# Experts' groups and the router's normalisation moved to ScalarE, and the seams around the last batch's dense experts rearranged

## The chip, the cores and the metric

The kernel runs on one core of one Trainium2 chip. A core has five engines with separate in-order queues: TensorE (PE, with its weight loads PEld) multiplies matrices, VectorE (DVE) and ScalarE (ACT) do elementwise work and read PSUM, GpSimd (POOL) does elementwise work in SBUF and issues indirect DMAs, and SyncE (SP) issues the other DMAs. They meet at semaphores. The metric is the device time of one execution in microseconds (us); the time before is the median of three runs.

## The reference

A hybrid layer of four sublayers on x of shape 4 x 1024 x 128 (4096 tokens, 128 features), each added back to x after a layer norm of its input:

```python
x = x + attn_a(layernorm(x))   # causal softmax attention, 16 heads of 64
x = x + ffn(layernorm(x))      # 32 experts, top 2
x = x + attn_b(layernorm(x))   # linear attention, 16 heads of 8
x = x + ffn(layernorm(x))      # the same experts again

def layernorm(x):
    return (x - mean(x)) / sqrt(var(x) + 1e-5)

def ffn(x):
    rw = softmax(x @ router_w.T)                 # 32 weights a token
    w = rw where it is one of the 2 largest, else 0
    return sum over e of (x * w[:, e]) @ expert_w[e]

def attn_b(x):
    q, k, v = x @ Wq.T, x @ Wk.T, x @ Wv.T
    g = sigmoid(x @ Wg.T + bg)
    qf, kf = softplus(q) * (g + 1e-6), softplus(k)
    kv_cum, z_cum = cumsum(kf x v), cumsum(kf)   # over the 1024 tokens
    return ((qf . kv_cum) / (qf . z_cum + 1e-6)) @ Wo.T
```

All of it is in float32.

## The kernel before

x stays in SBUF for the whole program, as 32 chunks of 128 tokens (x_sb; eight chunks a batch, four chunks a quarter q). Four stages follow one another.

**Softmax attention** (lines 477 to 834). A loop over 4 batches and 8 pairs of heads; for each pair eight units, one per chunk of queries. The function slot issues one unit's scores and, in between, later steps of earlier units. project returns a generator of six pieces (two halves of keys and queries, two pieces of values) that fill the slots of the pair before; for the very first pair all six are run ahead of the loop (lines 723 to 725). Sparse experts of a finished batch run beside it: experts (line 197) sorts tokens by expert through DRAM, and its last step, fetch (line 438), adds the results back with 16 indirect DMAs that POOL issues from a queue, one each time the queue is popped. At the end project_out (line 704) adds the last batch's output into x_sb chunk by chunk, and statistics (line 117) takes mean and variance of four chunks at a time and returns mean and reciprocal deviation.

**Dense experts of the last batch** (lines 1115 to 1145, names ending in _f). routed (line 851) prepares a quarter: normalised rows xn (VectorE, line 873), their transposes pxn (line 884), the copy xnT (line 885), router logits pl (line 892), softmax and the two largest weights, w. dense (line 928) then multiplies every token by all 32 experts. A block is a pair of chunks (c0 = 0 or 2) and eight groups g of four experts; each group takes two PSUM tiles of 512. For the groups in ACT_GROUPS (1, 4, 6) ScalarE multiplies by the weight into an SBUF tile t (line 966) and POOL adds the tiles of a chunk together (line 972), folding four experts into one at the end of a block (lines 990 and 991). For the other five groups VectorE multiplies and adds into x_sb straight from PSUM (line 978). settle (line 934) adds the folded partial sums to x_sb (line 937) when a later block has begun, and all that are left at the end of dense. Twice in each group dense calls next on the routing of the following quarter and beside(turn), so there are 16 turns in a block; for a quarter whose statistics are known, its routing is over within the first block.

Beside these blocks run the first two preparations of the linear stage, prepare (line 1018), for batch 0's chunks 0 to 3 and 4 to 7: statistics, reciprocal deviation rstd and negated product nb on POOL, normalised rows on ScalarE (line 1039), transposes, four projections pj (line 1057) with four ScalarE copies each, Exp, Sigmoid, Ln, and POOL's sums. In fill the two preparations advance in turn, and every fourth turn pops one item of the queue, which holds the fetches of batch 2's sparse experts.

**Linear attention** (lines 1147 to 1248). For each chunk u: cumulate (line 1158) multiplies kv by a triangular matrix into three PSUM banks, outputs (line 1175) makes the products m on VectorE, carry (line 1167) completes the running sum, finish divides, projects and adds. products (line 1095) makes the next chunk's kv on POOL. Preparations run 26 thirds of a chunk ahead.

**Experts after it** (lines 1250 to 1272, names ending in _s). Batch 0's quarters go through sparse experts beside dense on the quarters 2 to 7, twelve blocks. Here statistics are not known in advance, so routed takes them itself, with rstd on POOL (line 864), and its steps spread over the first block and half of the second. At the end of dense the results go out by DMA (line 940).

From line 847 on the program's order within each engine is that of the Python code (manual_schedule), so an instruction that waits holds everything that was written after it for the same engine.

Of the kernel before, what the change touches and what calls it, by code (L numbers as in the profile page):

```python
# [8 lines left out]
F32 = mybir.dt.float32  # L9
# [6 lines left out]
P = 128  # L16
# [4 lines left out]
def hybrid_kernel(  # L21
# [95 lines left out]
    def statistics(c0, n, nm):  # L117

        st = small.tile([P, n, nc.vector.BN_STATS_DIM], F32, tag=f"st{n}", name=f"st_{nm}")
        mv = small.tile([P, n, nc.vector.BN_AGGR_DIM], F32, tag=f"mv{n}", name=f"mv_{nm}")  # L120
        for c in range(n):
            nc.vector.bn_stats(st[:, c, :], x_sb[:, c0 + c, :])
            nc.vector.bn_aggr(mv[:, c, :], st[:, c, :])
        ve = small.tile([P, n], F32, tag=f"ve{n}", name=f"ve_{nm}")
        nc.vector.tensor_scalar_add(ve, mv[:, :, 1], LN_EPS)
        rstd = small.tile([P, n], F32, tag=f"rstd{n}", name=f"rstd_{nm}")
        nc.gpsimd.tensor_tensor(rstd, ve, mhalf[:, :n], ALU.pow)
        return mv, rstd
# [345 lines left out]

    sides, queue = [], []
    banks = [None]
    with attn as ph:
# [245 lines left out]
        cur, ahead = project(0, 0)  # L723
        for _ in ahead:
            pass
# [69 lines left out]
        for i, (b, pr) in enumerate(pairs):  # L795
# [10 lines left out]
            for k, ib in enumerate(ORDER):  # L806
# [12 lines left out]
                slot(u, (nm, ib - 1, twos[two], va, oT), k)  # L819
            if i + 1 < len(pairs):  # L820
                cur = nxt
# [9 lines left out]
        for c, _ in enumerate(project_out(*pend)):  # L831
            if c % 4 == 3:
                c0 = (B - 1) * NB + c - 3
                known.append(statistics(c0, 4, f"mf_{c0 // 4}"))

# [9 lines left out]
    ACT_GROUPS = (1, 4, 6)  # L845
# [5 lines left out]
    def routed(q, nm, pool, known=None):  # L851

        c0 = q * 4
        if known is None:
# [9 lines left out]
            nc.gpsimd.tensor_tensor(rstd, ve, mhalf[:, :4], ALU.pow)  # L864
            yield
            yield
            yield
        else:
            mv, rstd = known
        xn = rp.tile([P, 4, D], F32, tag="xn", name=f"xn_{nm}")  # L870
        xnT = rp.tile([P, 4 * P], F32, tag="xnT", name=f"xnT_{nm}")
        for c in range(4):
            nc.vector.tensor_scalar(
                xn[:, c, :], x_sb[:, c0 + c, :], mv[:, c, 0:1], rstd[:, c : c + 1],
                ALU.subtract, ALU.mult,
# [52 lines left out]
    def dense(nm_, qs, store, pool, mp, ps_e, known, beside):  # L928
# [16 lines left out]
        for i, q in enumerate(qs):  # L945
# [4 lines left out]
            for c0 in (0, 2):  # L950
                parts = [[], []]
                for g in range(E // 4):
# [9 lines left out]
                    if g in ACT_GROUPS:  # L962
# [32 lines left out]
        settle(0)  # L995
# [5 lines left out]

    lin = ExitStack()
# [3 lines left out]
    G = 4  # L1006
# [4 lines left out]
    tri, eps = mtri, epsn[:, :G]  # L1011
# [3 lines left out]

    feats = {}

    def prepare(t, pool):

        c0 = t * G  # L1020
        st = small.tile([P, G, nc.vector.BN_STATS_DIM], F32, tag="stl", bufs=2, name=f"st_l{t}")
        mv = small.tile([P, G, nc.vector.BN_AGGR_DIM], F32, tag="mvl", bufs=2, name=f"mv_l{t}")
        for c in range(G):
            nc.vector.bn_stats(st[:, c, :], x_sb[:, c0 + c, :])
            nc.vector.bn_aggr(mv[:, c, :], st[:, c, :])
            if c == 1:
                yield
        rstd = small.tile([P, G], F32, tag="rstdl", bufs=2, name=f"rstd_l{t}")
        nb = small.tile([P, G], F32, tag="nbl", bufs=2, name=f"nb_l{t}")
        nc.gpsimd.tensor_tensor(rstd, mv[:, :, 1], eps, ALU.add)  # L1030
        nc.gpsimd.tensor_tensor(rstd, rstd, mhalf[:, :G], ALU.pow)
        nc.gpsimd.tensor_tensor(nb, mv[:, :, 0], rstd, ALU.mult)
        nc.gpsimd.tensor_scalar(nb, nb, -1.0, None, ALU.mult)
        yield
        yield
        xn = lb.tile([P, G, D], F32, tag="xn", bufs=2, name=f"xn_l{t}")
        xnT = lb.tile([P, G * P], F32, tag="xnT", bufs=2, name=f"xnT_l{t}")
        for c in range(G):
            nc.scalar.activation(
                xn[:, c, :], x_sb[:, c0 + c, :], AF.Identity,  # L1040
                scale=rstd[:, c : c + 1], bias=nb[:, c : c + 1],
            )
        yield
        pt = pool.tile([P, 512], F32, tag="ps1", name=f"pxn_l{t}")
        for c in range(G):
            nc.tensor.transpose(pt[:, c * P : (c + 1) * P], xn[:, c, :], ident)
        nc.scalar.copy(xnT, pt)
        yield
        kq = lb.tile([P, G, 2 * P], F32, tag="kq", name=f"kq_{t}")
        y = lb.tile([P, G, 2 * P], F32, tag="y", bufs=2, name=f"y_{t}")  # L1050
        u = lb.tile([P, G, 2 * P], F32, tag="u", bufs=2, name=f"u_{t}")
        ln = lb.tile([P, G, 2 * P], F32, tag="ln", bufs=2, name=f"ln_{t}")
        gt = lb.tile([P, G, P], F32, tag="gt", bufs=2, name=f"gt_{t}")
        va = lb.tile([P, G, P], F32, tag="va", name=f"va_{t}")
        for c in range(G):
            pj = pool.tile([P, 512], F32, tag="ps1", name=f"pj_{t}_{c}")
            nc.tensor.matmul(
                pj, xnT[:, c * P : (c + 1) * P], wc.rearrange("p w d -> p (w d)"),
                start=True, stop=True,
            )  # L1060
            nc.scalar.activation(y[:, c, :], pj[:, : 2 * P], AF.Abs)
            nc.scalar.activation(kq[:, c, :], pj[:, : 2 * P], AF.Relu)
            nc.scalar.copy(gt[:, c, :], pj[:, 2 * P : 3 * P])
            nc.scalar.copy(va[:, c, :], pj[:, 3 * P :])
            if c == G - 1:
                nc.gpsimd.tensor_tensor(
                    gt, gt, bg_sb.unsqueeze(1).to_broadcast([P, G, P]), ALU.add
                )
            yield


        nc.scalar.activation(y, y, AF.Exp, scale=-1.0)
        nc.scalar.activation(u, y, AF.Copy, bias=1.0)
        yield
        yield
        nc.scalar.activation(gt, gt, AF.Sigmoid)
        yield
        yield
        nc.vector.scalar_tensor_tensor(y, u, 1.0, y, ALU.subtract, ALU.subtract)
        nc.scalar.activation(ln, u, AF.Ln)  # L1080
        yield
        yield
        yield
        for i in range(2):
            cols = slice(i * P, (i + 1) * P)
            nc.gpsimd.tensor_tensor(ln[:, :, cols], ln[:, :, cols], y[:, :, cols], ALU.subtract)
            nc.gpsimd.tensor_tensor(kq[:, :, cols], kq[:, :, cols], ln[:, :, cols], ALU.add)
            yield
        yield
        yield  # L1090
        q = kq[:, :, P:]
        nc.vector.scalar_tensor_tensor(q, gt, 1e-6, q, ALU.add, ALU.mult)
        feats[t] = (kq, va)
# [21 lines left out]
    with ExitStack() as ph:  # L1115
        mp = ph.enter_context(tc.tile_pool(name="mpf", bufs=12, reuse_waits="tile"))
# [3 lines left out]
        preps = [prepare(t, ps_f) for t in range(2)]  # L1120

        def fill(turn):

            if turn == 56:
# [5 lines left out]
            if turn % 4 == 3:  # L1130
# [5 lines left out]
        for _ in routed(qs[0], f"f_{qs[0]}", ps_f, known[0]):  # L1136
            next(preps[0], None)
        dense("f", qs, False, ps_f, mp, ps_e, known, fill)
# [8 lines left out]
    with lin as ph:  # L1147
# [80 lines left out]
        for u in range(NT + 4):  # L1228
# [15 lines left out]
            ahead(3 * u + 2)  # L1244
            if u == NT - 8:
# [3 lines left out]

    for _ in first:  # L1250
        pass
# [11 lines left out]
    with ExitStack() as ph:  # L1263
# [4 lines left out]
        dense("s", qs, True, ps_s, mp, ps_e, [None] * len(qs), pieces)  # L1268
# [36 lines left out]
```

## Time and profile before

| what | value |
|---|---|
| time, median of 3 runs (lowest, highest) | 2023.33 us (2021.16, 2025.43) |
| profiled execution: its time | 2022.32 us |
| its span, first to last instruction | 2020.6 us |
| mean granted TensorE clock | 0.980 |
| busy: PE, DVE, ACT, POOL | 1887.1, 1500.4, 1228.5, 1136.2 us |
| DMA, mean over the span | 31 GB/s |

The stages by the first and last instructions of their lines:

| stage | from | to |
|---|---|---|
| first scores to last residual add of softmax attention | 22.5 | 1479.7 |
| dense experts of the last batch, matmuls | 1495.5 | 1569.8 |
| linear attention, first to last running sum | 1577.0 | 1769.1 |
| dense experts after it, matmuls | 1773.4 | 2013.2 |

A row of the profile's timeline gives start, duration, engine, line, operation, the tiles written and read, shapes, and in brackets how long the engine had been idle and what ended that. A row of the table by stretches gives for each engine the busy time and the number of instructions, then the granted clock, the DMA share and the bandwidth. A float32 matmul is two passes, so a tile of 512 columns counts twice.

### The profile page before, as it was taken

To read this page: it belongs to the slowest core of one execution; us is meant where nothing else is said; L and a number is where in the kernel's file an instruction comes from. 1 tells how busy PE (TensorE), PEld (TensorE's weight loads), DVE (VectorE), ACT (ScalarE), POOL (GpSimd) and SP (SyncE) were. 2 spreads that over 40 slices of the span, in tenths; PEclk is the share of its full clock that TensorE was granted. 3 is DMA by queue.
4 is the path that set the end of the run, shared out by engine and by line. 5 is a ranking of instruction groups with operands and counts; after the bars stand their busy time and mean duration, and the time that the engine had idled before them with its cause. 6 is when DMAs were issued, how large, how long until landed. Compare 5 with 4: busy or idle time off the path is not lost.

```text
span 2020.6 us, 33597 instructions
## 1 busy us (share of the span) xinstructions
PE 1887.1 (93%) x10066; PEld 1052.0 (52%) x10066; DVE 1500.4 (74%) x4467; ACT 1228.5 (61%) x3889; POOL 1136.2 (56%) x2080
## 2 busy tenths in 40 slices
PE   6999999999999999999999999999979788888897
PEld 3555555555555655555565555555643344543453
DVE  5776776776787676778867776776748778978877
ACT  4766666766667566766766676676645466344433
POOL 3444444454666466556834954665438666537737
PEclk9999999999999999999999999999989899988999
DMA  7000000000002310000132100003311000000251
GB/s 215 1 1 1 1 1 1 1 1 1 1 12 79 108 21 12 1 1 1 45 107 57 21 1 1 1 13 93 101 45 13 6 0 1 0 1 12 62 147 47
DMA packets 111875, 62.54 MB, mean 31 GB/s; under 512 B 5552, under 2 KB 110160, under 8 KB 111568
## 3 DMA queue, kind: packets, MB, share of 16 engines
q1 hardware_dynamic: 101936, 50.43, 8.8%
q0 software_dynamic: 9472, 8.40, 2.1%
q8 instruction: 82, 1.34, 0.3%
q10 hardware_dynamic: 288, 1.57, 0.2%
q14 instruction: 97, 0.79, 0.1%
HBM read 35.60 MB, written 24.77 MB: 30 GB/s over the span
## 4 chain that ended last, share of the span: by engine, by line
PE 63%; DVE 17%; ACT 10%; POOL 7%; issue 3%; DMA 1%; SPq 0%; ACTq 0%; POOLq 0%; DVEq 0%
PE s L588 19%; PE po L694 10%; PE pt L677 10%; DVE nmx L597 5%; PE pe_s L956 4%; ACT p L622 4%; PE pw L709 3%; PE pk L537 3%; DVE x_sb L978 3%; ACT pT L681 2%; PE pe L417 2%; PE pv L551 2%; ACT p L627 1%; PE cum L1162 1%; PE cum L1170 1%
## 5 line engine op out<-in xcount | busy, mean ns | idle before, releaser
L597 DVE TENSOR_REDUCE nmx<-s 128x2 f32<-128x1024 f32 x512 | 604.5, 1220 | 214.5 <-PE s L588 206.2
L622 ACT ACTIVATE p<-s,nmx 128x512 f32<-128x512 f32 (+3 forms) x640 | 360.8, 575 | 309.6 <-DVE nmx L597 277.5
L588 PE MATMUL s<-kT,qT 64*128 64x512 f32 x2048 | 517.8, 619 | 7.8 <-ACT p L622 4.5
L664 POOL TENSOR_SCALAR p<-p,f,ri 128x512 f32<-128x512 f32 (+3 forms) x768 | 502.5, 670 | 0.9 <-issue 0.6
L677 PEld LDWEIGHTS pt<-ident,p 128*128 128x128 f32 x2304 | 250.0, 141 | 218.0 <-issue 90.4
L677 PE MATMUL pt<-ident,p 128*128 128x128 f32 x2304 | 336.0, 282 | 23.4 <-POOL rs L642 7.1
L681 ACT COPY pT<-pt 128x512 f32<-128x512 f32 (+3 forms) x768 | 324.1, 509 | 14.8 <-PE pt L677 10.4
L646 POOL TENSOR_TENSOR rs<-rs,f 128x2 f32<-128x2 f32 x256 | 51.8, 202 | 437.2 <-ACT f L613 407.7
L694 PE MATMUL po<-pT,va 128*64 128x256 f32 (+1 forms) x2560 | 291.1, 365 | 0.6 <-DVE oT L701 0.6
L588 PEld LDWEIGHTS s<-kT,qT 64*128 64x128 f32 x2048 | 173.1, 185 | 195.2 <-issue 95.0
L627 ACT ACTIVATE p<-s,nmx 128x128 f32<-128x128 f32 x512 | 180.3, 365 | 107.5 <-DVE nmx L597 104.8
L694 PEld LDWEIGHTS po<-pT,va 128*64 128x64 f32 x2560 | 167.0, 136 | 97.2 <-issue 32.6
L956 PE MATMUL pe_s<-we_sb,xnT_s 128*128 128x512 f32 x384 | 184.9, 630 | 9.2 <-ACT t_s L966 5.5
L978 DVE SCALAR_TENSOR_TENSOR x_sb<-pe_s,w_s,x_sb 128x128 f32<-128x128 f32 x480 | 129.8, 341 | 32.7 <-PE pe_s L956 31.3
L635 DVE SCALAR_TENSOR_TENSOR p<-p,qtri 128x128 f32<-128x128 f32 x512 | 145.3, 311 | 7.0 <-ACT p L627 3.7
L642 POOL TENSOR_TENSOR rs<-rs 128x2 f32<-128x2 f32 x192 | 43.8, 228 | 187.4 <-DVE ri L655 187.4
L622 ACT ACTIVATION_READ_ACCUMULATOR p<-s,nmx 128x1 f32 x640 | 138.9, 217 | 0.0
L956 PEld LDWEIGHTS pe_s<-we_sb,xnT_s 128*128 128x128 f32 x384 | 74.0, 202 | 100.2 <-issue 58.4
L966 ACT ACTIVATE t_s<-pe_s,w_s 128x128 f32<-128x128 f32 x288 | 78.4, 380 | 50.2 <-PE pe_s L956 47.1
L714 DVE TENSOR_TENSOR x_sb<-pw,x_sb 128x128 f32<-128x128 f32 x128 | 36.9, 289 | 79.5 <-PE pw L709 79.1
L972 POOL TENSOR_TENSOR t_s<-t_s,t_s 128x512 f32<-128x512 f32 x48 | 60.2, 1272 | 60.8 <-ACT t_s L966 60.1
L709 PE MATMUL pw<-wo_sb,oT 128*128 128x128 f32 x512 | 84.5, 290 | 1.8 <-DVE x_sb L714 1.0
(302 smaller groups left out, 2677.0 us busy)
## 6 DMA issues: line engine op xcount, KB each, us to landing
xs<-xs_d SPq DMA_DIRECT2D x33, 256.0 KB, 3.0
ys_d<-ys SPq DMA_DIRECT2D x33, 256.0 KB, 2.4
we<-_ffn_expert_weights_dram SPq DMA_DIRECT2D x24, 256.0 KB, 3.8
xs_d<-zero SPq DMA_DIRECT2D x2, 3008.0 KB, 18.4
we<-_ffn_expert_weights_dram SPq DMA_DIRECT2D x45, 64.0 KB, 1.8
xs_s<-xs_d SPq DMA_DIRECT2D x11, 256.0 KB, 3.7
ys_d<-ys_s SPq DMA_DIRECT2D x11, 256.0 KB, 2.8
we_sb<-_ffn_expert_weights_dram SPq DMA_DIRECT2D x4, 512.0 KB, 6.1
```

The source lines that it names most:

```text
L588: nc.tensor.matmul(st[:, h, :], self.qT[rows, self.ib * P : (self.ib + 1) * P], self.kT[rows, j * 512 : (j + 1) * 512], start=True, stop=True,
L597: nc.vector.tensor_reduce(self.nmx[:, i, :], self.s[i], AX.X, ALU.max, negate=True)
L622: nc.scalar.activation(self.p[h][:, at : at + m * P], self.s[i][:, h, : m * P], AF.Exp, bias=bias, accum_out=self.rs[:, i, h : h + 1],)
L627: nc.scalar.activation(self.p[h][:, at + m * P : at + (m + 1) * P], self.s[i][:, h, m * P : (m + 1) * P], AF.Exp, bias=bias,)
L635: nc.vector.scalar_tensor_tensor(d, d, 1.0, qtri, ALU.mult, ALU.mult, accum_out=self.rs[:, 2, h : h + 1])
L664: nc.gpsimd.tensor_scalar(w, w, self.f[:, i, h : h + 1], self.ri[:, h : h + 1], ALU.mult, ALU.mult,)
L677: nc.tensor.transpose(pt[:, c * P : (c + 1) * P], self.p[h][:, (g + c) * P : (g + c + 1) * P], ident,)
L681: nc.scalar.copy(self.pTs[h][:, g : g + m, self.col : self.col + P], pt[:, : m * P].rearrange("p (c i) -> p c i", c=m),)
L694: nc.tensor.matmul(po[h * DH : (h + 1) * DH, c0:256], va[:, jb, h, :], pTs[h][:, jb, c0:], start=(jb == 0), stop=(jb == n - 1),)
L709: nc.tensor.matmul(pw[:, :P], oTs[i][:, c * P : (c + 1) * P], wo_sb[:, pr, :], start=(i == 0), stop=(i == len(prs) - 1),)
L956: nc.tensor.matmul(pe, xnT[:, c * P : (c + 1) * P], we_sb[:, 4 * g : 4 * g + 4, :].rearrange("p e d -> p (e d)"), start=True, stop=True,)
L978: nc.vector.scalar_tensor_tensor(xs, pe[:, e * D : (e + 1) * D], w[:, c, 4 * g + e : 4 * g + e + 1], xs, ALU.mult, ALU.add,)
```

## The change

Six edits.

1. Normalised rows of the router (line 873) go from VectorE to ScalarE, as rstd * x + nb. POOL computes nb in two small instructions, in statistics and in routed.

```diff
-        return mv, rstd
+        nb = small.tile([P, n], F32, tag=f"nb{n}", name=f"nb_{nm}")
+        nc.gpsimd.tensor_tensor(nb, mv[:, :, 0], rstd, ALU.mult)
+        nc.gpsimd.tensor_scalar(nb, nb, -1.0, None, ALU.mult)
+        return rstd, nb
...
         for c in range(4):
-            nc.vector.tensor_scalar(
-                xn[:, c, :], x_sb[:, c0 + c, :], mv[:, c, 0:1], rstd[:, c : c + 1],
-                ALU.subtract, ALU.mult,
+            nc.scalar.activation(
+                xn[:, c, :], x_sb[:, c0 + c, :], AF.Identity,
+                scale=rstd[:, c : c + 1], bias=nb[:, c : c + 1],
             )
             if c == 1:
                 yield
```

2. In the second block of every quarter, four groups instead of three go to ScalarE.

```diff
-    ACT_GROUPS = (1, 4, 6)
+    ACT_GROUPS = ((1, 4, 6), (1, 3, 5, 7))
...
-                    if g in ACT_GROUPS:
+                    if g in ACT_GROUPS[c0 // 2]:
```

3. At the start, the two value pieces of the first pair of heads run after the first two slots.

```diff
-        cur, ahead = project(0, 0)
-        for _ in ahead:
-            pass
+        cur, rest_ = project(0, 0)
+        for _ in range(4):
+            next(rest_)
...
                 slot(u, (nm, ib - 1, twos[two], va, oT), k)
+                next(rest_, None)
```

4. prepare is defined ahead of the attention (its body is unchanged; it takes its PSUM tiles through a small class that looks up the pool of the moment). Its first three steps, the statistics with rstd and nb, run for both preparations between the last residual adds, and the first one's next eight steps run at chosen steps of the first quarter's routing, no longer at each.

```diff
+    class Bank:
+        def tile(self, *a, **k):
+            return banks[0].tile(*a, **k)
+
+    preps = [prepare(t, Bank()) for t in range(2)]
...
         for c, _ in enumerate(project_out(*pend)):
             if c % 4 == 3:
                 c0 = (B - 1) * NB + c - 3
                 known.append(statistics(c0, 4, f"mf_{c0 // 4}"))
+            elif c < 7:
+                next(preps[c // 4])
...
-        for _ in routed(qs[0], f"f_{qs[0]}", ps_f, known[0]):
-            next(preps[0], None)
-        dense("f", qs, False, ps_f, mp, ps_e, known, fill)
+        for i, _ in enumerate(routed(qs[0], f"f_{qs[0]}", ps_f, known[0])):
+            if i in (0, 4, 8, 9, 10, 11, 12, 13):
+                next(preps[0])
+        settle = dense("f", qs, False, ps_f, mpf, ps_e, known, fill)
```

5. In fill, the queue is popped every third turn instead of every fourth, and the first kv of the linear stage is issued at turn 46 instead of 56.

```diff
-            if turn == 56:
+            if turn == 46:
                 for p in preps:
                     for _ in p:
                         pass
                 feats["kv"] = products(0)
             next(preps[turn % 2], None)
-            if turn % 4 == 3:
+            if turn % 3 == 2:
```

6. dense returns settle and no longer calls it at its end. After the last batch's blocks the four chunks that are left settle in the linear stage, after chunk u = 1; the pool of the tiles t, now of 13 and not 12, stays open until the linear stage is over. After the final blocks settle is called at once, as before.

```diff
-        settle(0)
+        return settle
...
+    shares = ExitStack()
+    mpf = shares.enter_context(tc.tile_pool(name="mpf", bufs=13, reuse_waits="tile"))
...
             ahead(3 * u + 2)
+            if u == 1:
+                settle(0)
...
+    shares.close()
...
-        dense("s", qs, True, ps_s, mp, ps_e, [None] * len(qs), pieces)
+        dense("s", qs, True, ps_s, mp, ps_e, [None] * len(qs), pieces)(0)
```

## The prediction

> **What bounds the kernel now.** First the granted clock: one core, 0.980, so idle shows up as time and not as throttling alone. Then the busy shares by engine: TensorE 93%, VectorE 74%, ScalarE 61%, POOL 56%. An average over stages with different limits, so next a table by stretches. I cut the dense experts into their blocks: one block is a pair of 128-token chunks and eight groups of four experts.
>
> ```profile
> core 0: us, PE busy (x) PEld busy (x) DVE busy (x) ACT busy (x) POOL busy (x), PEclk, DMA share, GB/s
> 1495.47:1520.79 25.32, 20.95 (x56) 9.70 (x54) 19.16 (x68) 18.89 (x49) 14.83 (x14) 0.87 0.05 6
> 1520.79:1541.68 20.89, 17.85 (x35) 7.41 (x34) 17.71 (x57) 14.49 (x40) 15.85 (x15) 0.84 0.11 13
> 1541.68:1555.42 13.74, 13.74 (x34) 5.90 (x32) 11.03 (x40) 7.31 (x28) 13.11 (x12) 1.00 0.08 11
> ...
> 1569.77:1591.23 21.46, 8.21 (x13) 4.02 (x13) 15.40 (x26) 0.34 (x2) 17.37 (x18) 0.69 0.08 9
> ```
>
> The four blocks of the last batch (three shown) need 13.7 us where nothing disturbs TensorE. The first two take 25.3 and 20.9, and the 21.5 us after the last block hold 8.2 us of TensorE work. The timeline there, by engine, says why:
>
> ```profile
> 1577.00 4.21 PE L1162 MATMUL cum<-kv,mtri 128*128 128x384 f32 x6 [7.23 <-POOL kv L1100]
> 1587.23 4.21 PE L1170 MATMUL cum<-kv,rest 128*128 128x384 f32 x6 [6.02 <-DVE m L1182]
> ...
> 1582.52 0.79 DVE L937 TENSOR_TENSOR x_sb<-x_sb,t_f 128x128 f32<-128x128 f32 x1 [5.21 <-POOL t_f L991]
> ...
> 1583.65 2.12 POOL L1100 TENSOR_TENSOR kv<-kq,va 128x1024 f32<-128x1024 f32 x1
> ```
>
> POOL is late. VectorE stands in the settling adds (L937) until POOL has folded the ScalarE partial sums, and the products m of the linear stage queue behind it. In the last stage, the same table for five of its twelve blocks:
>
> ```profile
> 1840.02:1857.65 17.63, 14.25 (x35) 5.89 (x34) 17.01 (x64) 6.93 (x26) 13.63 (x24) 1.00 0.05 16
> 1857.65:1876.28 18.63, 17.80 (x44) 7.71 (x45) 17.02 (x66) 9.20 (x32) 16.17 (x24) 0.91 0.07 25
> 1876.28:1891.23 14.95, 14.26 (x35) 6.00 (x35) 13.95 (x60) 9.28 (x34) 12.11 (x19) 1.00 0.16 49
> 1891.23:1914.81 23.58, 19.40 (x62) 9.81 (x60) 19.96 (x64) 8.27 (x27) 16.09 (x20) 0.93 0.29 85
> ...
> 1966.32:1980.13 13.81, 13.81 (x34) 6.16 (x34) 12.81 (x58) 6.71 (x25) 10.95 (x13) 1.00 0.16 45
> ```
>
> No single engine bounds it: VectorE does in 1840 (17.0 of 17.6), TensorE in 1966, and in 1891 TensorE idles 4.2 us for this:
>
> ```profile
> 1902.31 1.04 POOL L864 TENSOR_TENSOR rstd_s<-ve_s,mhalf 128x4 f32<-128x4 f32 x1 [2.21 <-DVE ve_s L862]
> ...
> 1904.21 2.21 DVE L873 TENSOR_SCALAR xn_s<-x_sb,mv_s,rstd_s 128x128 f32<-128x128 f32 x4
> ...
> 1904.74 0.33 PE L884 MATMUL pxn_s<-ident,xn_s 128*128 128x128 f32 x1 [2.24 <-DVE xn_s L873]
> 1905.96 0.99 PE L884 MATMUL pxn_s<-ident,xn_s 128*128 128x128 f32 x3 [0.89 <-DVE xn_s L873]
> ```
>
> The next quarter's transposes wait for its normalised rows, and the expert matmuls queue behind them.
>
> **The change, part by part**, against the profiled run's own 2022.32 us (span 2020.6 and 1.7 around it), which is 1.0 below the median.
>
> *Start, -1.0.* Eight value matmuls (20.63 to 22.50) leave the path to the first scores. Scores still need the second half of qT, copied until 21.43, so they start at 21.45 and not 22.50. The moved matmuls fit TensorE's waits in the first slots (0.76, 0.90, 1.65 us around 25 us). The two va copies of 0.58 land between exponentials; without cover they cost 1.2. Range -1.9 to +1.2.
>
> *Attention to dense experts.* Eight pairs of statistics, 0.42 each, go between the last residual adds. VectorE is 3.4 us longer there but had gaps (1.23 us is one), and the normalisation leaves it. Today ScalarE's copy of xnT_f starts at 1488.27, long after its transposes, since it queues behind xn_l, which waits for POOL until 1486.7. With POOL's chain started earlier I get the copy at about 1486, router logits at 1488 instead of 1494.7, and, as the exponential no longer queues behind Exp and u (2.1 us), the first weights near 1495 instead of 1502.6. The expert weights' four SP transfers, issued at 1479.44, may go a microsecond later; they are done long before.
>
> *That gain does not reach the end; POOL does.* I count what POOL must finish before kv of the second linear chunk, today ready at 1585.77. From 1508.42 that is 77.35 us, less 3.8 idle (1533.3 to 1537.1) and about 1.5 of small waits: 72. New: minus 1.9 (rstd and nb of the second preparation, now earlier), minus 3.4 (two of the fifteen fetches at 1.56 and 0.15 issue, which go while POOL is empty), plus 2.6 (two of L1086/L1087, until now at 1503 to 1506), plus four adds at a pitch of 1.24: 74.3. It begins when ScalarE finishes the first half of group 4. From the end of the first preparation's copies (1493.7, three earlier than now) ScalarE has Exp and u 2.1, two lots of four normalisations 3.3 (L1039: four in 1.65), Sigmoid with its table 1.9, group 1 2.17, two copies 1.2, Ln with its table 2.34, two projections 1.9, half a group 1.1: 1509.7. POOL then ends at 1584.0, at 1585.7 with the small waits back. kv of the first chunk is now issued before the last block's adds, and VectorE no longer settles first, so the second chunk's cum starts at 1585.7 instead of 1591.23: **-5.5**. Had POOL no waits and an earlier start, -11; if the fetches, now every third turn, push the adds back until ScalarE lacks t tiles (13), +3.
>
> *Linear stage, -2.5.* Four normalisations leave VectorE: 3.79 and 0.57, of which TensorE waited 2.18 visibly; VectorE is busy 98% around there, so I take 3.5. Four settling adds come in, 0.28 each if undisturbed, 2.2 if one meets POOL's kv: +1.0. Range -4.4 to +2.8. That the partial sums' pool lives through this stage, and that prepare stands elsewhere in the code, issues nothing.
>
> *Last stage.* Six second blocks give one group each to ScalarE: minus 8 x 0.267 = 2.1 us VectorE, plus eight at 0.27 ScalarE and two POOL adds at 1.27. ScalarE is busy 101 of 240 us there, POOL 140, so both have cover. TensorE idles 10.1 us in the five second blocks before the last. I take 3.4 at 1840, 0.7 at 1876 and a third of the 6.0 at 1795 and 1915, where sparse experts' copies mix in: -6.1. Against it stand the normalised rows. New chain from the end of rstd: nb 0.62, two rows 0.86, *group 4's eight evictions 2.17, which stand between the rows in ScalarE's order*, two rows 0.86, transposes 0.45: 4.96. Today's, at 1785.46, 1827.55, 1869.86 and 1903.35, took 3.7, 5.1, 2.3 and 3.6. That is +1.3, -0.1, +2.6, +1.4; the fifth waits for sparse weights: +5.2. Behind the wait in ScalarE's queue are those evictions, and their banks. The very end: the last group goes to ScalarE, its second half is done 2014.35, adds 2.5 from 2013.5, folding 2.64: 2018.65 instead of 2016.65, +2.0, less 1.0 as the sixth group no longer waits 1.99 for VectorE. Stage: **+0.1**, between -12 (all idle gone, rows free) and +7.
>
> Sum: -1.0 - 5.5 - 2.5 + 0.1 = -8.9, so 2013.4, and with the 1.0 to the median **2014.4**.
>
> A rule against it: the Trainium skill, GPSIMD Engine Reference, Key points, says POOL shares its SBUF interfaces with VectorE and disturbs VectorE instructions with two SBUF inputs or in a two-port mode. The trace agrees: L937, two SBUF inputs, takes 0.276 to 5.477 us and ends with POOL's instruction. With a quarter more POOL adds per quarter of a batch it would add a quarter of the settling adds' excess, (593 - 284) ns x 22 / 4 = 1.7 us; the sum would be -7.2.
>
> **Rivals.** (a) *POOL starvation*: the crossing gives +1.5 instead of -5.5. For it: POOL was busy 57 of 74 us in those blocks and gets 5 more. Against: its idle time is early. Sum -1.9: 2021.4, no change. (b) *Slower: ScalarE held at the rows.* In each first block ScalarE stands from group 1 until nb, with evictions behind it. If every one of five costs the 2.6 of 1869.86 (13.0), second blocks turn out TensorE-bound like 1966 (0) and the tail costs 2.0, the stage is +15 and the sum +6.0: 2029.3. It decides from +13 in the stage, 2.2 us a block. Against: VectorE enters the first blocks less late. (c) *VectorE was everything*: stage -12, crossing -8, so -23.5: 1999.8. Against: 1966 is TensorE-bound already.
>
> **Numbers.** Forecast (2004 to 2019, its own range) 0.52; (a) 0.17; (b) 0.20; (c) 0.11. Within 0.2% is 2019.3 to 2027.4, about what this measurement can tell from no change. Faster takes the forecast, (c) and a little of (a): 0.64; same 0.15, mostly (a); slower 0.21, (b) and a little of (a). The range 2001 to 2028 leaves out half of (c) and over half of (b).
>
> **What will show it.** First scores at 21.4; first expert eviction about 1495; second cum near 1585, its wait on POOL's kv, no L937 before m; no L873 on VectorE, L1170's 2.18 wait gone; second blocks at 14 to 15 us; TensorE waits before the turned rows longer, now for ScalarE. I am wrong if the second cum stays near 1591, or the last stage (1773 to 2013, 239.7 us) moves over 7 us either way.

## The result and the profile after

The changed kernel takes 2027.84 us (median of 11 runs, 2026.8 to 2029.19) against 2023.33 of the kernel before in the same session (11 runs, 2019.4 to 2025.93): a ratio of 1.0023, 95% interval 1.0014 to 1.0032. It is slower by some 4.6 us, where 8.9 faster was forecast. The profiled execution took 2027.25 us (span 2025.5, mean granted clock 0.975).

The busy line of its page, engine by engine:

```profile
PE 1890.8 (93%) x10066; PEld 1056.1 (52%) x10066; DVE 1464.1 (72%) x4371; ACT 1257.5 (62%) x3985; POOL 1158.2 (57%) x2112
```

VectorE lost 36 us of work and ScalarE and POOL gained 29 and 22, as the edits intend; the sum of the work is no guide to the time. The table by stretches of the changed kernel, cut at the same matmuls as before:

```profile
core 0: us, PE busy (x) PEld busy (x) DVE busy (x) ACT busy (x) POOL busy (x), PEclk, DMA share, GB/s
1493.54:1519.27 25.73, 22.16 (x58) 10.43 (x56) 14.12 (x51) 21.37 (x59) 11.17 (x9) 0.87 0.07 9
1519.27:1540.36 21.09, 16.99 (x33) 6.89 (x32) 17.16 (x56) 15.03 (x40) 19.85 (x18) 0.84 0.11 13
1540.36:1560.70 20.34, 16.82 (x33) 7.07 (x32) 11.29 (x38) 8.28 (x31) 18.87 (x17) 0.83 0.11 13
1574.60:1586.72 12.12, 3.87 (x13) 1.93 (x11) 5.23 (x16) 1.80 (x8) 11.96 (x13) 0.78 0.00 0
1836.56:1850.74 14.18, 13.98 (x35) 5.98 (x34) 13.56 (x56) 6.60 (x25) 11.77 (x22) 1.00 0.07 19
1850.74:1877.17 26.43, 18.64 (x45) 8.12 (x45) 17.28 (x62) 15.80 (x53) 22.98 (x33) 0.87 0.07 23
1877.17:1891.77 14.60, 14.09 (x34) 5.87 (x34) 13.57 (x50) 7.93 (x31) 13.21 (x21) 1.00 0.14 45
1891.77:1914.43 22.66, 18.24 (x61) 9.11 (x61) 16.88 (x61) 10.53 (x35) 15.76 (x20) 1.00 0.30 85
1966.03:1979.84 13.81, 13.81 (x34) 6.16 (x34) 12.78 (x54) 7.26 (x28) 10.85 (x13) 1.00 0.14 39
1994.76:2016.12 21.36, 16.57 (x33) 6.74 (x31) 12.55 (x45) 7.27 (x27) 17.45 (x17) 0.84 0.20 56
```

The fourth block of the last stage (1836.56) went from 17.63 to 14.18, as forecast, and the fifth behind it from 18.63 to 26.43. There POOL is busy 22.98 of 26.43. Here is the timeline of that fifth block, with the same steps from rstd to the transposes that the lines of before show for a later one:

```profile
1865.20 1.06 POOL L961 TENSOR_TENSOR rstd_s<-ve_s,mhalf 128x4 f32<-128x4 f32 x1
1865.24 0.40 ACT L372 ACTIVATE xw_s<-xn_s,wt_s 128x128 f32<-128x128 f32 x1 [3.00 <-DMA xs_d<-xw_s,row_s]
...
1866.90 0.88 ACT L973 ACTIVATE xn_s<-x_sb,nb_s,rstd_s 128x128 f32<-128x128 f32 x2 [1.25 <-POOL nb_s L964]
...
1867.45 0.71 PE L984 MATMUL pxn_s<-ident,xn_s 128*128 128x128 f32 x2 [2.61 <-ACT xn_s L973]
1867.68 2.15 ACT L1066 ACTIVATE t_s<-pe_s,w_s 128x128 f32<-128x128 f32 x8
...
1869.68 0.91 ACT L973 ACTIVATE xn_s<-x_sb,nb_s,rstd_s 128x128 f32<-128x128 f32 x2
...
1870.26 0.85 PE L984 MATMUL pxn_s<-ident,xn_s 128*128 128x128 f32 x2 [2.10 <-ACT xn_s L973]
```

Three things hold ScalarE one after the other: a scattered buffer xw (L372), nb from POOL, and its own evictions (L1066) between the second and the third row. TensorE waits 2.61 and 2.10 us in its order. At the crossing, second cum and the products m:

```profile
1586.72 4.21 PE L1183 MATMUL cum<-kv,mtri 128*128 128x384 f32 x6 [8.25 <-POOL kv L1121]
...
1588.41 0.56 DVE L1203 TENSOR_TENSOR m<-cum,kq 128x384 f32<-128x384 f32 x1 [8.30 <-PE cum L1183]
...
1589.69 0.56 DVE L1203 TENSOR_TENSOR m<-cum,kq 128x384 f32<-128x384 f32 x1 [0.72 <-PE cum L1183]
```

It starts 4.51 us earlier than before, waiting for POOL's kv and no settling add, but the six matmuls take 4.21 and not 2.10, and VectorE gets its operands at a pitch of 1.28.

Where the time went, as the difference of positions to the kernel before: first cum -2.6, second -4.5, third -2.15, last one -6.1, first expert matmul of the last stage -6.3, its sixth block +0.9, the end +4.9. The last stage with its tail took 258.4 us and not 247.2: **+11.2** where +0.1 was forecast. Without the tail it is 249.0 against 239.7, which is over the 7 us that the prediction named as a sign that it is wrong.

### The profile page after: what moved, and what is told of

It reads as the page before. It is cut to its first block, busy times and chain, and to the rows that moved or that the text cites. A ratio compares the mean times of both kernels' runs of the same rounds, so it can differ in the third digit from the quotient of the medians.

```text
span 2025.5 us, 33613 instructions
## 1 busy us (share of the span) xinstructions
PE 1890.8 (93%) x10066; PEld 1056.1 (52%) x10066; DVE 1464.1 (72%) x4371; ACT 1257.5 (62%) x3985; POOL 1158.2 (57%) x2112
## 4 chain that ended last, share of the span: by engine, by line
PE 62%; DVE 14%; POOL 9%; ACT 9%; issue 4%; DMA 1%; SPq 0%; ACTq 0%; POOLq 0%; DVEq 0%
PE s L681 19%; PE po L787 10%; PE pt L770 10%; DVE nmx L690 6%; PE pe_s L1056 5%; ACT p L715 3%; PE pw L802 3%; PE pk L630 3%; POOL x_sb L442 2%; ACT pT L774 2%; DVE x_sb L1078 2%; PE cum L1183 2%; PE cum L1191 2%; PE pe L420 2%; PE pv L644 1%
## 5 line engine op out<-in xcount | busy, mean ns | idle before, releaser
L1056 PE MATMUL pe_s<-we_sb,xnT_s 128*128 128x512 f32 x384 | 185.9, 635 | 14.2 <-DVE x_sb L1078 12.0
L1078 DVE SCALAR_TENSOR_TENSOR x_sb<-pe_s,w_s,x_sb 128x128 f32<-128x128 f32 x432 | 116.7, 340 | 47.7 <-PE pe_s L1056 47.5
L1066 ACT ACTIVATE t_s<-pe_s,w_s 128x128 f32<-128x128 f32 x336 | 90.9, 384 | 42.3 <-PE pe_s L1056 39.4
L1072 POOL TENSOR_TENSOR t_s<-t_s,t_s 128x512 f32<-128x512 f32 x60 | 75.2, 1276 | 59.6 <-ACT t_s L1066 59.5
```

What stands on the lines that cost most here:

```text
L1056: nc.tensor.matmul(pe, xnT[:, c * P : (c + 1) * P], we_sb[:, 4 * g : 4 * g + 4, :].rearrange("p e d -> p (e d)"), start=True, stop=True,)
L1078: nc.vector.scalar_tensor_tensor(xs, pe[:, e * D : (e + 1) * D], w[:, c, 4 * g + e : 4 * g + e + 1], xs, ALU.mult, ALU.add,)
```

## Experiments

Two theories for these 11 us: the *rows* on ScalarE, or the *fourth group's* POOL adds. All ratios are to runs of the kernel before on the same chip, with a 95% interval; its own median lies between 2022.57 and 2025.09 us from one group of runs to the next. A difference of two ratios from different chips is uncertain by 0.0013 to 0.0018, some 3 us. Contrasts of kernels that ran on one chip are taken from the medians. Block times come from one profiled execution of each kernel.

### Rows back, groups back, both back

```diff
 # rows_back, in routed (quarters 3 to 7; quarter 2 falls into the linear stage)
-            nc.scalar.activation(xn[:, c, :], x_sb[:, c0 + c, :], AF.Identity, scale=rstd[...], bias=nb[...])
+            nc.vector.tensor_scalar(xn[:, c, :], x_sb[:, c0 + c, :], mv[:, c, 0:1], rstd[...], ALU.subtract, ALU.mult)
 # groups_back, in dense
-                    if g in ACT_GROUPS[c0 // 2]:
+                    if g in ACT_GROUPS[0 if store else c0 // 2]:
```

> The changed kernel, but in the last stage the normalised rows of quarters 3 to 7 are VectorE's again, with no nb on POOL; quarter 2, whose rows fall into the linear stage, and the last batch stay on ScalarE; the fourth group stays. The last stage (first to last expert matmul and the tail) cost 11.2 us more than in the kernel before. Theory 1, the rows did it (ScalarE's order puts evictions behind rows that wait): the rows cost 11.2 + 5.1 = 16, the groups keep my 5.1 of gain, so 2027.8 - 16 = 2011.5, 2010 to 2015. Theory 2, the fourth group's POOL adds did it (scatters, fetches and folding late): the rows are worth no more than my 5.2, so 2022 to 2028.

> The changed kernel, but all blocks of the last stage give ScalarE the three groups 1, 4 and 6 again; the rows stay on ScalarE and the last batch keeps its fourth group. Theory 1 (rows): the groups were a gain of 5.1 that is given up, so slower than the changed kernel: 2029 to 2033. Theory 2 (POOL adds): the loss goes except for my 5.2 of the rows: 2027.8 - 6 = 2021.8, or down to 2017 if the rows cost nothing.

> Both at once: the last stage is that of the kernel before, and only the edits ahead of it (the start, the crossings, quarter 2's rows in the linear stage) are left. Either theory: 2027.8 - 11.2 = 2016.6, within 2 us. If it is the sum of the two single effects, rows and groups do not disturb each other; if the single effects add up to less than 11, each is enough to make the stage late; more than 2 us above 2016.6 would mean that the stage is slower because it starts earlier or with other work left over, and neither edit did it.

Measured: rows back 2023.1 us, 0.9994 (0.9985 to 1.0003); groups back 2024.38, 0.9998 (0.9989 to 1.0007); both back 2017.08, 0.9963 (0.9951 to 0.9975). Both single edits are a loss, of 7.3 us (rows) and 6.0 (groups) beside the other undone. Theory 1 is out. Theory 2, which left the rows my 5.2, named the range in which rows back came, and groups back came 2.6 above its 2021.8: the rows cost somewhat more than 5.2. My -5.1 for the groups had the wrong sign. Undone alone they give 5.9 and 5.1 by the ratios, undone together 12.1, so within the uncertainty they add up, and both back came within 0.5 of its 2016.6: the stage is not slower for another reason.

Block by block, groups alone (rows_back against both_back, from the starts of the matmuls): second blocks -6.4 in sum (forecast -6.1), the fifth block 24.7 against 18.7, the last block 21.1 against 17.4, the tail 9.4 against 7.5, and -1.0 in the sum of the rest. The gain is there, and the blocks behind it give it back. Rows alone (groups_back against both_back): first block 23.9 against 21.7, fifth 22.7 against 18.7, the others the same within 1.8. Single blocks differ by as much without a change in them: the ninth takes 25.6 us in the kernel before and 27.7 in both_back.

### Where the fourth group loses: the scatters

In the fifth block of rows_back, the timeline of ScalarE and of the POOL work it waits for, and then the same two waits in both_back, with three groups:

```profile
1855.44 2.50 POOL L1080 TENSOR_TENSOR t_s<-t_s,t_s 128x512 f32<-128x512 f32 x2
...
1858.10 1.05 POOL L362 DMA_INDIRECT xs_d<-xw_s,row_s  x1 [0.16 <-issue]
...
1860.52 0.40 ACT L372 ACTIVATE xw_s<-xn_s,wt_s 128x128 f32<-128x128 f32 x1 [2.73 <-DMA xs_d<-xw_s,row_s]
...
1864.21 0.40 ACT L372 ACTIVATE xw_s<-xn_s,wt_s 128x128 f32<-128x128 f32 x1 [3.29 <-DMA xs_d<-xw_s,row_s]
1864.52 2.16 ACT L1074 ACTIVATE t_s<-pe_s,w_s 128x128 f32<-128x128 f32 x8
```

```profile
1862.12 0.40 ACT L372 ACTIVATE xw_s<-xn_s,wt_s 128x128 f32<-128x128 f32 x1 [0.95 <-DMA xs_d<-xw_s,row_s]
1863.98 0.40 ACT L372 ACTIVATE xw_s<-xn_s,wt_s 128x128 f32<-128x128 f32 x1 [1.46 <-DMA xs_d<-xw_s,row_s]
```

The adds of the fourth block's last group (2.50) stand ahead of the third scatter (L362, the indirect DMA that sorts rows by expert); ScalarE waits for a buffer that the scatter frees, and group 4's evictions behind it in its queue come 3.5 us after their matmuls. More buffers, and three groups in the very last block:

```diff
-                    t = xo.tile([P, D], F32, tag="xw", bufs=8, ...)
+                    t = (came or xo).tile([P, D], F32, tag="xw", bufs=16 if came else 8, ...)
 # rows_back_xw16_l3, besides
+                    if g in ACT_GROUPS[0 if q == qs[-1] and store else c0 // 2]:
```

> The kernel with the rows back on VectorE and four groups in the second blocks (2023.1), but the sparse experts of the last stage get 16 buffers xw instead of 8. In that kernel ScalarE's xw waited 2.73 and 3.29 us in the fifth block for scatters that POOL issues behind the fourth group's adds, and that block was 6.1 us longer than with three groups, more than the 4.1 that the block before it had gained. Theory A, ScalarE is held by the late scatters through the eight buffers: the fifth block loses its 6.1, 2017 to 2018.5. Theory B, POOL's own lateness (rstd and the folding behind the scatters) holds the block: less than 2 us off, 2021 to 2023.

> As before it, and the very last block gives ScalarE three groups again. My tail term was +2.0 less 1.0; measured with four groups the last block and the tail took 4.4 us more than with three. If the four groups are to blame there (later fetches for the sparse results, the last group's second half, two more adds before the last folding): 4.4 off the kernel with 16 buffers, 2013 by theory A. If the earlier blocks only push the loss to the end (what POOL owes is paid there anyway): under 1.5 off.

Measured: 2018.68 us, 0.998 (0.9971 to 0.9989), and 2019.14, 0.9981 (0.9972 to 0.999). Sixteen buffers bring about 2.8 us by the ratios, hardly clear of their uncertainty, and 1.75 of the fifth block's 6.1 in the profile (24.74 to 22.99): ScalarE's waits for the scatters are gone, but rstd is still late behind two scatters (1862.08, its operand since 1859.98), and VectorE's rows with it. Between the theories: the buffers were a part. The rest, by this timeline, is POOL's order; no run moved the adds behind the scatters to show it. Three groups in the last block alone gave nothing.

### Where it loses: the last sparse results

```diff
+                    if g in ACT_GROUPS[0 if q in qs[-2:] and store else c0 // 2]:
```

> The kernel with the rows on VectorE and four groups in second blocks (2023.1, 0.9994 of the kernel before), but with three groups in the last two quarters. Taking the fourth group from the last block alone changed nothing: that block was as long as before (23.6) with VectorE 7.35 us at the last sparse results. From the first to the last fetch POOL took 35.1 us with the fourth group and 32.6 with three, which are two adds of the block before the last quarter. If these adds, through the fetches, are what holds VectorE in the last block: its wait falls from 7.3 to about 3, the last block and the tail lose 4 to 4.5, a ratio of 0.997. If the last block's length comes from the sparse experts' own transfers: wait and time as they are, a ratio over 0.9985.

Three groups in the last two quarters, all else as in rows_back. Measured: 2016.58 us, 0.9971 (0.9962 to 0.998), 4.6 below rows_back by the ratios. VectorE's wait before the last sparse results are added (L474), in the changed kernel, and then in this one (rows_back itself had 7.38, both_back 3.13):

```profile
2007.25 0.89 DVE L474 TENSOR_TENSOR x_sb<-x_sb,y_s 128x512 f32<-128x512 f32 x1 [7.33 <-DMA y_s<-ys_d,row_s]
```

```profile
1999.43 0.84 DVE L474 TENSOR_TENSOR x_sb<-x_sb,y_s 128x512 f32<-128x512 f32 x1 [3.15 <-DMA y_s<-ys_d,row_s]
```

Last block and tail fell from 30.5 in rows_back to 25.6. The last block alone had given nothing, so this loss hangs on the fourth group of the block before the last quarter, and not on the length of the sparse experts' own transfers. That it acts through the fetches behind the two adds is read from the wait.

### The order of the rows

```diff
             nc.scalar.activation(xn[:, c, :], x_sb[:, c0 + c, :], AF.Identity, scale=rstd[...], bias=nb[...])
-            if c == 1:
+            if c == 1 and known is not None:
                 yield
+        if known is None:
+            yield
```

The four rows of the last stage thus stand together, ahead of group 4's evictions; all else as in groups_back, then as in the changed kernel.

> The kernel with three groups in all blocks of the last stage and the rows on ScalarE (1.0 of its ratio to the kernel before), but in the last stage the four rows stand together ahead of group 4's evictions in ScalarE's order, where two stood behind them. Rows cost 6.2 to 6.7 us against VectorE's, in the first block (2.2) and the fifth (4.1) alone. My step's price was rstd to nb 0.62, two rows, group 4's evictions 2.17, two rows, transposes: if that order is the price, the second transposes' wait (2.11) goes, about 2.2 in each of the two blocks: 3 to 4.5 off, a ratio of 0.998. If ScalarE is held by nb's lateness on POOL, or group 4's banks by the 0.86 that they come later: under 1 off, a ratio over 0.999.

> The changed kernel with one thing different: in the last stage the four rows stand together ahead of group 4's evictions. With three groups this took the ratio from 0.9998 to 0.9954. If the fourth group's cost is POOL's order alone (scatters, fetches and folding behind its adds), it stays at 4 to 6 us here: a ratio of 0.9975 to 0.9985. If it was the crowding of ScalarE at the rows, the fourth group now costs nothing or gains: 0.9955 or less.

Measured: 2011.98 us, 0.9954 (0.994 to 0.9968), and with four groups 2021.69, 0.9982 (0.9973 to 0.9991). The order alone is worth 0.0044 of the time, 8.9 us, twice what I expected, and the rows on ScalarE now cost nothing against VectorE's (0.9963). The fourth group still costs 0.0028, 5.7 us, as forecast for the case that it does not hang on the rows. The first block of the stage, groups_back first, then with the rows together; columns as in any timeline:

```profile
1782.37 0.88 ACT L973 ACTIVATE xn_s<-x_sb,nb_s,rstd_s 128x128 f32<-128x128 f32 x2 [6.64 <-POOL nb_s L964]
...
1785.73 0.86 PE L984 MATMUL pxn_s<-ident,xn_s 128*128 128x128 f32 x2 [1.97 <-ACT xn_s L973]
...
1786.38 6.34 PE L1056 MATMUL pe_s<-we_sb,xnT_s 128*128 128x512 f32 x8
```

```profile
1781.00 1.65 ACT L973 ACTIVATE xn_s<-x_sb,nb_s,rstd_s 128x128 f32<-128x128 f32 x4 [6.64 <-POOL nb_s L964]
...
1781.55 1.48 PE L986 MATMUL pxn_s<-ident,xn_s 128*128 128x128 f32 x4 [0.51 <-ACT xn_s L973]
...
1782.87 3.61 PE L1058 MATMUL pe_s<-we_sb,xnT_s 128*128 128x512 f32 x8
```

The second wait (1.97) is gone, and the same eight expert matmuls after it (four tiles, which the profile counts twice, as it shows 384 for the 192 of the stage) take 3.61 us and not 6.34. Here the clock had already dropped before the rows, after a wait of 2.00 for VectorE. pops4 (below), whose rows are split too, has it at 0.94 until the wait for the second pair; its stretches before and after that wait, the figure behind POOL's being the clock (PEclk), and then the same in groups_back_rows4, with the rows together:

```profile
1776.77:1782.70 5.93, 3.26 (x9) 1.38 (x9) 5.79 (x27) 3.69 (x12) 3.48 (x5) 0.94 0.00 1
1782.70:1788.26 5.56, 5.56 (x17) 2.81 (x17) 1.29 (x6) 2.87 (x9) 2.78 (x3) 0.76 0.00 0
```

```profile
1779.08:1782.87 3.79, 3.11 (x9) 1.24 (x9) 3.69 (x18) 1.87 (x6) 1.45 (x3) 1.00 0.01 2
1782.87:1787.12 4.25, 4.25 (x17) 2.34 (x17) 3.41 (x15) 4.25 (x17) 3.27 (x3) 1.00 0.00 0
```

In the four profiled kernels with split rows that last stretch ran at 0.60, 0.76, 0.61 and 0.61, in the four with the rows together at 1.00, and the block took 22.2 to 24.0 against 18.8 us. In pops4 and kv_early the clock was full until the second wait; there the wait came with 3.4 and 6.8 us at half clock, and the block was 3.4 and 4.9 us longer than with the rows together. In the other two, groups_back and the changed kernel, the half clock had begun before it, so what the second wait alone cost them is not shown.

The clock does not always follow. The second wait (1.96 to 2.11 us) stands in the first, third, fifth and seventh block of each of the four kernels. In the 5 us behind it the clock was below full in 12 of these 16, in four of them already before it, and 1.00 in four: in the seventh block of three of them, and in pops4's third, where the wait and the 5 us behind it read:

```profile
1824.37 0.71 PE L984 MATMUL pxn_s<-ident,xn_s 128*128 128x128 f32 x2 [2.10 <-ACT xn_s L973]
...
1824.37:1829.37 5.00, 4.95 (x16) 2.69 (x16) 0.35 (x1) 3.37 (x11) 4.40 (x4) 1.00 0.00 0
```

In the profiles the order of the rows also shortened the third block (24.3 us in groups_back, 18.8 with the rows together) and lengthened the second (21.2, 23.5).

The seven kernels of the last stage side by side (profiled us; rows by S, ScalarE, or V, VectorE). The profiled execution took 5.8 us less than the kernel's median in rows4_four and 2.6 less in groups_back_rows4, and 2.3 more in both_back, so the ratio and not the stage's time ranks them:

| kernel | rows | groups | ratio | stage and tail | first block | fourth | fifth | last | tail |
|---|---|---|---|---|---|---|---|---|---|
| before | V | 3 | 1 | 247.2 | 21.5 | 17.6 | 18.6 | 18.7 | 7.4 |
| both_back | V | 3 | 0.9963 | 247.5 | 21.7 | 17.6 | 18.7 | 17.4 | 7.5 |
| rows_back | V | 4 | 0.9994 | 251.8 | 21.7 | 14.2 | 24.7 | 21.1 | 9.4 |
| groups_back | S, split | 3 | 0.9998 | 253.6 | 23.9 | 17.7 | 22.7 | 18.7 | 7.5 |
| changed | S, split | 4 | 1.0023 | 258.4 | 24.0 | 14.2 | 26.4 | 21.4 | 9.4 |
| groups_back_rows4 | S, together | 3 | 0.9954 | 239.4 | 18.8 | 18.4 | 19.0 | 17.3 | 7.5 |
| rows4_four | S, together | 4 | 0.9982 | 248.4 | 18.8 | 15.4 | 23.5 | 21.1 | 9.4 |

### The crossing to the linear stage

```diff
 # pops4, in fill
-            if turn % 3 == 2:
+            if turn % 4 == 3:
 # kv_early, in fill; the loop takes this kv in place of products(1)
+            if turn == 47:
+                feats["kv1"] = products(1)
 # kv3, on both_back; the loop issues products(u + 1) for u >= 2 alone
-                feats["kv"] = products(0)
+                feats["kv"] = {u: products(u) for u in range(3)}
+            if turn in (36, 38):
+                next(third)          # prepare(2, Bank()), left to the loop after these two steps
...
-            if u == 1:
+            if u == 3:
                 settle(0)
```

> The changed kernel, but kv of the second linear chunk is issued at turn 47, ahead of the POOL adds of the last block, and the third chunk's in the second chunk's turn as now. My crossing stopped at 1586.7 for that kv. If POOL's order of work is all that holds TensorE there: second cum at about 1579 and not 1586.7, with warm clock, third at 1587 to 1588 (kv behind six adds and the folding) and not 1594.5: 6 to 7.5 us off, 2020 to 2022. If the count of POOL's work is what holds the stage (it has to be done at some time before the products can flow): third or fourth cum is late instead, under 2 us off, 2026 to 2028.

> The changed kernel with the queue of fetches popped at every fourth turn again. In the last batch's third block VectorE waited 3.72 us for POOL's sums of kq, which were late behind fetches, and the fourth block began 5.3 us later than in the kernel before though the first had begun 1.9 earlier. If the faster fetches cost that: the fourth block starts 4 to 6 us earlier. My count for the second cum (POOL's whole work is the same) then still says no change of the end: second cum at 1585 to 1588, 2026 to 2029. If the 6.6 us are lost for the stage: second cum 3 to 5 us earlier, 2023 to 2025.

> The kernel with both back in the last stage (2017.1), and at the crossing to the linear stage: kv of the first three linear chunks are issued at turn 47 ahead of the last block's adds, the third preparation's statistics and POOL part at turns 36 and 38, and the settling waits until after the fourth chunk. The single kv ahead brought the second cum from 1586.7 to 1581.0 (at a start 2.7 later) but the third was late, since VectorE stood in the settling adds until POOL had folded (1589.8) and kv was behind three more POOL steps. If POOL's order and that settle are what costs the crossing: second, third and fourth cum follow at 5 to 6 us, the linear stage starts its steady pace some 7 us earlier, 2009 to 2011. If POOL's total work is the limit there: fourth cum late by as much, 2016 to 2018.

Measured: kv_early 2025.5 us, 1.0005 (0.9996 to 1.0014); pops4 2022.73, 1.0002 (0.9993 to 1.0011); kv3 2010.1, 0.9939 (0.9926 to 0.9953).

kv_early: second cum at 1580.99, third at 1598.33, 21.2 us after the first (20.1 in the changed kernel). VectorE stood in settle until 1589.8, and kv came behind the third preparation's rstd on POOL. Only the wait moved. kv3 moves these too (the timeline gives its POOL and its running sums):

```profile
1573.88 6.81 POOL L1130 TENSOR_TENSOR kv<-kq,va 128x1024 f32<-128x1024 f32 x3
...
1583.08 7.40 POOL L1081 TENSOR_TENSOR t_f<-t_f,t_f 128x512 f32<-128x512 f32 x6
...
1587.55 2.10 PE L1194 MATMUL cum<-kv,mtri 128*128 128x384 f32 x6
...
1595.06 2.20 PE L1194 MATMUL cum<-kv,mtri 128*128 128x384 f32 x6 [2.29 <-POOL kv L1130]
```

Three kv, then what POOL owes the last batch (7.40 and the folding), and only the fourth cum waits, 2.29. From the last attention matmul to the first expert matmul of the last stage it takes 279.4 us, against 286.8 in both_back. So these 7 us (4.9 by the ratios) were the price of the order, and not of POOL's count of work. kv, the third preparation and the settling moved together; their shares are not shown.

pops4: the fourth block of the last batch started 3.2 us earlier, second cum 0.6 later, as the count had said. Its median is lower than the changed kernel's all the same; in the profile that is 3.6 us in the last stage, whose code is the same in both. In the first block there the clock was 0.94 and 0.76 where the changed kernel had 0.61 and 0.60 at the same matmuls. Ahead of the stage TensorE waited 1.59 us in both; behind that the clock was 0.90 over the first 10.7 us in pops4 and 1.00 in the changed kernel, and the next wait, for VectorE, was 0.86 and 2.00. Why the clock fell there in one and not in the other is open.

> The fastest so far (three kv ahead, settle after the fourth chunk, last stage as before; 0.9939 of the kernel before) with the queue popped at every fourth turn in the last batch. Popping later brought the fourth block of the last batch 3.3 us forward, and the second cum 0.6 back, as POOL owed the fetches behind the block. With kv ahead of what POOL owes, the 3.3 should now reach the linear stage: 2 to 3.5 off, a ratio of 0.9925. If the fetches left over hold the settling or the fourth kv: nothing gained.

> The same with three groups for ScalarE in the last batch's second blocks too. By the count of POOL's work (two adds of 1.24 fewer in each of two blocks) 2.5 to 5 us less is owed; VectorE gets eight evictions, 2.1, more in each. If POOL bounds these blocks: 1 to 4 us faster than with four groups. If VectorE does: 1 to 4 slower.

Measured: 0.9956 (0.9942 to 0.9969) and 0.9968 (0.9957 to 0.998), no gain over kv3. With the later fetches the fourth cum came at 1596.3, after 6.56 us of waiting for kv, behind a fetch, two adds and the folding. With three groups (kv3_pops4_f3) the last batch's fourth block took 24.1 us and not 13.9.

### The best version

```diff
 # best1: kv3 with the rows on ScalarE, together, in the last stage, three groups there
 # best2: the rows together in the last batch too
```

> Rows on ScalarE with all four together, three groups in the last stage, and the crossing with three kv ahead and the settling after the fourth chunk. If the cures add up: 0.9939 with the rows back on VectorE, and rows together against VectorE's 0.9954 to 0.9963, so 0.993, some 14 us under the kernel before. In the profile the last stage should take 232 to 240 us and the way from the last attention matmul to the first expert matmul 280 (294.0 in the kernel before). If the last stage's gain came from the moment at which it starts: 0.995.

> The same with the rows together in the last batch's dense experts too, whose first and only such rows stand in the first of its four blocks (25.7 us long). If TensorE's wait for the turned rows is in the way there as in the last stage: 1 to 3 us less. If that block is bounded by the linear preparation's work on ScalarE: no difference, within 1.

Measured: best1 2006.97 us, 0.991 (0.9897 to 0.9924); best2 2004.92, 0.9896 (0.9881 to 0.9912), against 2025.09 of the kernel before beside them. They beat the kernel before by 18 and 20 us, and the changed one by 23 and 26 by the ratios; the two differ by less than their intervals, so whether the rows together help in the last batch is not shown. best1's crossing took 278.9, its last stage 232.9. The cures add up: 0.991 where their sum was 0.993, within the intervals.

## Why the prediction was wrong

**The step that failed** is the fourth group's term in the last stage: "minus 6.1" for the second blocks, and for the end "+2.0, less 1.0". The 6.1 were right (6.4 without the rows' edit). What I put at nothing was POOL's two adds a block, with "POOL 140" of 240 us as cover. That is an average: in the fifth block POOL is the queue that sparse scatters, rstd and the folding share, busy 16.2 of 18.7 us even with three groups, and near the end the fetches stand in it. Behind the adds came the scatters late (+6.1 in the fifth block) and the fetches (+3.7 in the last block, where I had hoped for -1.0). With the tail's +1.9 and -1.0 in the rest the term is +4.3 in the profile, and +5 to +6 by medians and ratios in three pairs, for a forecast -5.1. These 10 us are most of the miss of 13.5 (8.9 faster forecast, 4.6 slower measured). None of the rivals had this step: (a) looked for POOL at the crossing alone. That it is POOL's adds, and not the eight evictions that ScalarE takes over in the same block, is read from the timelines, in which ScalarE stands 2.73 and 3.29 us for scatters and VectorE 7.38 for fetched results; no run separates the two.

**Rows, +5.2:** measured 7.3 beside three groups, by the ratios 5.9 beside four. The chain was the right one, with the evictions in ScalarE's order between the rows: taking them out removed the whole cost (8.9, with the uncertainty above). What the chain left out is the clock, which was often low behind the wait. The rival *ScalarE held at the rows* had that mechanism and named 15 for the stage, but with second blocks that gain nothing, and every first block alike; against VectorE's rows the cost lay in the first and the fifth.

**Crossing, -5.5:** the count on POOL held (second cum forecast at 1585.7, measured 1586.72), but half of it went in the next chunk, since TensorE came out of 8.25 us of idleness at half pace: -2.15 at the third cum. **Linear stage, -2.5:** -4.2 from third cum to the last stage; the four settling adds, which I priced at +1.0, met nothing (0.88 for the four). **Start, -1.0:** the profile after shows it (first scores 21.51), but kernels with the same start show 21.5 to 23.1, so it cannot be told from chance; by the end of the attention nothing was left (its last matmul ended 1.1 us later). In the profile -2.15, -4.2 and the last stage's +11.2 make the +4.9 of the end. None of these three edits was undone alone.

On the Trainium skill's rule (GPSIMD Engine Reference, Key points, on the SBUF interfaces that POOL and VectorE share): from the kernel before to the changed one the 24 settling adds of the last stage rose from 567 to 607 ns each, 1.0 us, but the rows moved there too. Between kernels that differ in the fourth group alone their sum rose by 3.0 us (both_back 13.8, rows_back 16.7), 2.9 (groups_back 11.7, changed 14.6) and 4.5 (groups_back_rows4 14.3, rows4_four 18.8), more than the 1.7 of the estimate. 2.9 of it fell each time in the eleventh block, which took 0.5 to 0.6 longer, and 1.1 in the fifth, which took 3.7 to 6.1 longer. The rule pointed the right way; how much of these microseconds reached the end is not shown, and in the fifth block the loss is three to five times as large.

## What to carry to other kernels

Before work goes to an engine "with cover", list what stands behind it in that engine's queue in that block, and who waits for each: the share of the span says nothing of it. When four small instructions are spread between longer ones in program order, ask whether their consumer needs them all; putting them together was worth more (8.9 us) than any move between engines here. What is owed to nobody soon (partial sums, settling) belongs behind what the next stage starts with.

## What was not expected of the hardware

A short wait of TensorE can cost more than itself, and what it costs is not fixed by the code. Where the clock was full until the wait of some 2.1 us for the second rows (first block of pops4 and kv_early), it then stood at half for 3.4 and 6.8 us, and the block was 3.4 and 4.9 us longer than without the wait. The same wait left the clock at 1.00 in four blocks of 16. And the same matmuls, with the same code ahead of them in the stage, ran at 0.61 in one kernel and at 0.94 in another, 24.0 and 22.2 us for the block, so profiles of one stage differ by some 3 us where nothing in it was changed.
